# First stage of a two-layer kernel: latents in bursts of 32-row tiles, p turned in 64-row halves, division by eight heads, shorter FP4 rounding, a new step order

## The chip, the core and the metric

The kernel runs on one core of a Trainium2 chip. The metric is the device time of one execution in microseconds (us). TensorE (PE) multiplies, and its weight loads (PEld) are listed apart; VectorE (DVE), ScalarE (ACT) and GpSimd (POOL) work elementwise; SyncE (SP) issues most DMAs. TensorE writes only to PSUM, of which there are eight banks of 512 float32 columns by 128 partitions.

## What is computed

Two layers with a layer norm after each half, all in float32, on x of 16 batches x 512 tokens x 256 channels. Cut to what matters:

```python
# layer 0, attention: 16 heads of 16, lifted to 32 "latent" channels
qkv = x @ c_attn_w.T + c_attn_b ; q, k, v = heads(split(qkv))
q_lat = q @ q2l_w.T + q2l_b ; k_lat = k @ kv2l_w.T + kv2l_b ; v_lat = v @ kv2l_w.T + kv2l_b
q_lat = q_lat * cos + rotate_half(q_lat) * sin        # the same for k_lat
att = softmax(causal((q_lat @ wqk_w.T + wqk_b) @ k_lat.T * 32**-0.5))
y = (att @ v_lat) @ l2o_w.T + l2o_b                    # heads side by side
x = layernorm(x + y @ cproj_w.T + cproj_b)
# layer 0, FFN: each linear has its input and its weight rounded to FP4 in blocks of 16
#   scale = max(max|block| / 6, 1e-12); q = nearest of (0, .5, 1, 1.5, 2, 3, 4, 6) * sign * scale
x = layernorm(x + fp4_linear(silu(fp4_linear(x, w_gate)) * fp4_linear(x, w_up), w_down))
# layer 1: a recurrence over 512 tokens (state = tanh(state @ tanh(a) + x_t @ b)), then a gated FFN
```

## The kernel before

**Stages.** The first stage does attention and the FP4 FFN of layer 0, batch by batch, and writes rows of x to DRAM (`xs`). The second stage reads them back and runs the recurrence with the rest of layer 1 beside it.

**Order.** TensorE's order is the order of the program text. The other engines' instructions are ordered ahead of time by the framework's own scheduler, which may move an instruction, a DMA issue too, far ahead when nothing holds it. Attention runs in 16 x 12 slots: a slot is a batch, a group g of four heads, and one of three sets n of query blocks (`BLOCKS`: block 3, of 512 keys; block 2, of 384; blocks 1 and 0, of 256 and 128). In a slot the kernel

- forms the scores of four heads (`scores`: four products with 32 rows, each head in its own 32-row tile of TensorE and its own PSUM bank). DVE adds the mask and finds the minimum in one pass (tiles p and nm);
- runs the exponentials on ACT (`exponentials`), two heads late (`LAG = 2`);
- turns the p of the slot before, head by head, with 128x128 transposes (`turn`, tiles ps_pt and pT); ACT copies them to SBUF;
- after the third set multiplies with the values (`weighted`, tile py, four column tiles of 32) and, one slot later, divides by the sums (`divide`: DVE reciprocal rc, POOL widens it to rcx, TensorE turns it, ACT copies, DVE multiplies).

Between these, `half_slot` (eight times a slot) takes steps from a list written by hand (`PLAN`, and `PLAN_0`, `PLAN_1`, `PLAN_15` for the first, second and last batch): H heads, L latents, V values, O output projection, Q FP4 of x, U and D the FFN's two halves, W the FFN weights. "U-1.0" is the up half of token block 0 of the batch before. `TIME` holds a cost for each step, and steps are paced by it over the 96 half slots of a batch. `vector_step` hands one more piece of a waiting FP4 rounding to DVE at each half slot.

**Latents.** `latents(b, g)` has three steps for one group: q and k (two products of 64 rows and 128 columns, in the two row halves), q and k with swapped pairs (the same with bdqs and bdks), and the product with w1 (ps_qf). DVE multiplies by cos and sin, POOL adds the two, ACT adds the bias.

**PSUM.** `mm` hands out seven banks in a ring; an eighth (`ps_y`) holds py.

**FP4.** `fp4`: block maximum (L205), scale (L206), reciprocal (L207), x by the reciprocal (L210), two passes for the rounding constant (L214, L215), addition (L218), then subtraction and the product with the scale, on POOL in most calls (L219, L220).

**Weights of the recurrence.** `recurrent_weights` (28 small DMAs, five larger ones, a tanh on ACT) is called in the text at batch 2; its memory is its own, and in the profile its DMAs are issued from 17 us on.

## Time and profile before

| | |
|---|---|
| time, median of 3 runs | 2539.11 us (2538.06 to 2540.24) |
| the profiled execution: span from the first to the last instruction | 2543.7 us; no other time of that execution is recorded |
| PE, DVE, ACT, POOL busy | 2412.0, 1925.8, 1621.3, 1035.4 us |
| first score; last score | 31.7 us; 1748.2 us |
| first step of the recurrence | 1816.1 us |
| granted TensorE clock, 31 to 132 us; 354 to 1284 us | 0.87; 1.00 |

The rows of the profile name a line, an engine, an operation, its tiles and shape, how many there were, the busy time and the mean duration of one in ns, and the idle time of the engine before them with what ended it. A float32 product is two records on TensorE (two passes), a transpose one. Records of TensorE overlap, so that the distance from one start to the next says more than a duration.

### The profile page before, as it was taken

The numbers are of one execution on the slowest core, as the hardware profiler recorded it, in microseconds if no ns is written. First come the engines' busy times: TensorE is split into PE (matmuls) and PEld (weight loads), VectorE is DVE, ScalarE is ACT, GpSimd is POOL, SyncE is SP. The second block draws the span as 40 slices with busy tenths as digits, with TensorE's granted clock in tenths as the row PEclk, the third lists the DMA queues.
The fourth block names the chain that finished last, engine by engine and source line by source line (L and its number), as shares of the span: only waits on it lengthen the run. The fifth ranks groups of instructions, "written<-read, shape, count | busy, mean of one in ns | idle before, by whom it ended". The sixth has DMA issues, their size and how long they took to land.

```text
span 2543.7 us, 73791 instructions
## 1 busy us (share of the span) xinstructions
PE 2412.0 (95%) x28802; PEld 1712.7 (67%) x28802; DVE 1925.8 (76%) x5492; ACT 1621.3 (64%) x5536; POOL 1035.4 (41%) x1642
## 2 busy tenths in 40 slices
PE   7789999999999999999999999998799999999998
PEld 4455666666666666666666666655678888888885
DVE  4867888788888888888888888867756666666666
ACT  4656676676766666666666666654366666666664
POOL 4322333333333333333333333332445555555554
PEclk8889999999999999999999999989899999999999
DMA  3000000000000000000000000000111111111100
GB/s 117 24 9 6 12 24 14 16 16 12 24 14 16 16 12 24 14 16 16 12 24 14 16 14 6 16 14 9 43 32 39 37 40 41 40 38 39 36 28 27
DMA packets 58015, 61.30 MB, mean 24 GB/s; under 512 B 7873, under 2 KB 53058, under 8 KB 57666
## 3 DMA queue, kind: packets, MB, share of 16 engines
q1 hardware_dynamic: 56802, 55.54, 7.0%
q8 instruction: 226, 3.70, 0.6%
q14 instruction: 123, 1.01, 0.1%
q10 hardware_dynamic: 864, 1.05, 0.1%
HBM read 39.79 MB, written 16.78 MB: 22 GB/s over the span
## 4 chain that ended last, share of the span: by engine, by line
PE 51%; DVE 29%; ACT 10%; POOL 5%; issue 3%; DMA 1%; ACTq 0%; DVEq 0%; POOLq 0%; SPq 0%
PE u L1076 8%; DVE p L546 5%; PE ps_pt L569 5%; PE u L1036 5%; ACT p L559 4%; PE S L534 3%; PE ps_d L164 3%; DVE q_q L210 3%; ACT pT L571 3%; PE pg L164 3%; PE pu L164 2%; PE ps_h L449 2%; DVE q_sc L205 2%; DVE q_q L218 2%; PE ps_a L916 2%
## 5 line engine op out<-in xcount | busy, mean ns | idle before, releaser
L559 ACT ACTIVATE p<-p,nm 128x512 f32<-128x512 f32 (+3 forms) x1024 | 570.4, 562 | 492.3 <-DVE nm L546 488.3
L1084 ACT ACTIVATE hist<-u 64x64 f32<-64x64 f32 x2048 | 447.1, 218 | 237.4 <-PE u L1076 151.4
L546 DVE CUSTOM_DVE_ANT_0 p<-S,mask 128x512 f32<-128x512 f32 (+3 forms) x1024 | 442.9, 484 | 50.9 <-PE S L534 50.4
L1076 PEld LDWEIGHTS u<-hist,ta 128*64 128x64 f32 x8176 | 367.7, 138 | 119.9 <-ACT hist L1084 41.5
L569 PEld LDWEIGHTS ps_pt<-ident,p 128*128 128x128 f32 x2560 | 302.0, 142 | 217.3 <-issue 107.1
L571 ACT COPY pT<-ps_pt 128x384 f32<-128x384 f32 (+1 forms) x768 | 374.2, 517 | 62.3 <-PE ps_pt L569 62.1
L569 PE MATMUL ps_pt<-ident,p 128*128 128x128 f32 x2560 | 396.3, 280 | 4.5 <-DVE nm L546 3.0
L1076 PE MATMUL u<-hist,ta 128*64 128x32 f32 x8176 | 394.4, 218 | 4.6 <-ACT hist L1084 4.5
L219 POOL TENSOR_TENSOR q_q<-q_q,q_m 128x704 f32<-128x704 f32 (+1 forms) x140 | 164.1, 1172 | 372.2 <-DVE q_q L218 361.5
L534 PE MATMUL S<-kc,qr 32*128 32x512 f32 (+3 forms) x2048 | 224.1, 475 | 10.5 <-ACT qr L488 7.9
L1036 PE MATMUL u<-xt,wb 128*64 128x64 f32 x4128 | 224.9, 231 | 5.1 <-issue 5.0
L559 ACT ACTIVATION_READ_ACCUMULATOR p<-p,nm 128x1 f32 x1024 | 199.8, 195 | 0.0
L164 PE MATMUL ps_d<-wdT,hT 128*128 128x256 f32 x732 | 173.1, 386 | 13.9 <-DVE nm L546 12.1
L164 PE MATMUL pg<-wgT,xqT 128*128 128x352 f32 x512 | 177.9, 471 | 6.5 <-DVE nm L546 5.1
L483 POOL TENSOR_TENSOR qc<-qc,qs 128x512 f32<-128x512 f32 x64 | 81.5, 1273 | 235.5 <-DVE qs L482 221.1
L164 PE MATMUL pu<-wuT,xqT 128*128 128x352 f32 x512 | 173.7, 462 | 1.0 <-DVE nm L546 1.0
L1036 PEld LDWEIGHTS u<-xt,wb 128*64 128x64 f32 x4128 | 166.7, 140 | 10.3 <-issue 5.5
L600 PEld LDWEIGHTS py<-pT,vpad 128*32 128x32 f32 x5120 | 138.7, 110 | 47.0 <-issue 30.3
L600 PE MATMUL py<-pT,vpad 128*32 128x128 f32 x5120 | 162.6, 274 | 7.8 <-ACT pT L571 7.5
L164 PEld LDWEIGHTS ps_d<-wdT,hT 128*128 128x128 f32 x732 | 135.4, 192 | 37.6 <-DVE nm L546 15.4
L86 POOL TENSOR_SCALAR ve<-mv 128x2 f32<-128x2 f32 (+1 forms) x160 | 31.1, 194 | 312.4 <-DVE mv L94 309.7
L585 POOL COPY rcx<-rc 128x256 f32<-128x256 f32 x64 | 40.3, 630 | 286.9 <-DVE rc L583 260.9
(167 smaller groups left out, 4648.8 us busy)
## 6 DMA issues: line engine op xcount, KB each, us to landing
xT<-in_xT_dram SPq DMA_DIRECT2D x16, 512.0 KB
x<-in_x_dram SPq DMA_DIRECT2D x16, 512.0 KB
xs<-x SPq DMA_DIRECT2D x64, 128.0 KB
x<-xs SPq DMA_DIRECT2D x32, 256.0 KB
xm<-xs SPq DMA_DIRECT2D x32, 256.0 KB
out_dram<-o SPq DMA_DIRECT2D x64, 128.0 KB
w<-in_w_down_dram SPq DMA_DIRECT2D x2, 352.0 KB
w<-in_w_gate_dram SPq DMA_DIRECT2D x5, 128.0 KB
```

What stands on the lines that cost most here:

```text
L164: nc.tensor.matmul(dst, left, right, start=start, stop=stop)
L219: last.tensor_tensor(q, q, m, ALU.subtract)
L483: nc.gpsimd.tensor_tensor(of[k], of[k], x, ALU.add)
L534: nc.tensor.matmul(S[h][:, at : at + w], q[rs, i * P : i * P + P], k[rs, :w], start=True, stop=True,)
L546: nc.vector.tensor_tensor_reduce(out=p[:, own], in0=S[h][:, own], in1=mask[:, T - (i + 1) * P :], scale=1.0, scalar=-MASKED, op0=ALU.add, ...
L559: nc.scalar.activation(p[:, own], p[:, own], AF.Exp, bias=nm[:, u : u + 1], scale=-1.0, accum_out=sum_of[b, g][:, cb, half, h : h + 1],)
L569: nc.tensor.transpose(ps[:, at : at + P], p[:, at : at + P], ident)
L571: nc.scalar.copy(pT[:, :w], ps[:, :w])
L600: nc.tensor.matmul(py[q * 32 : q * 32 + 32, PLACE[i][1], :], vpad[b % 2][:, j, g * 4 + h, :], pt, start=j == 0 and h % 2 == 0, stop=j == i ...
L1036: nc.tensor.matmul(u[rs, k, par:n:2, bs : bs + 16], wb[:, g * 2 + k, par, half, rs], xt[:, g, at : at + n - par : 2, :], start=par == 0 an ...
L1076: nc.tensor.matmul(into[cs, :, c, :], ta[:, t % 2, g * 2 + k, cs], own[:, :, c, :], start=False, stop=True, skip_group_check=True,)
L1084: nc.scalar.activation(state[g][rs, :, r * 32 : r * 32 + 32].rearrange("p k (s b) -> p k s b", s=2), u[rs, :, t - t0, :] .rearrange("p k ( ...
```

## The change

- *Latents.* Steps are for a whole batch. `queries` (two steps, L): a spread, `spread`, of eight products of 32 rows and 64 columns into four banks; each bank times cos and times sin (eight DVE products); then 32 products of 32 rows and 32 columns that sum w1 with the cos part and w1s (new, a DMA) with the sin part into four banks, and four ACT additions of the bias. `keys` (two steps, K): a spread times cos, then a spread of the swapped weight times sin, added on POOL. bdqs and q2lbs go; the columns of wqk and the bias cabk for k are laid out anew, cabk by eight small DMAs.
- *Turning p.* Two heads at a time, each 128x128 block as two transposes of 64 rows, the row halves in different banks; four ACT copies a slot as before. All eight of a head pair's halves stand together, ahead of the slot's scores.
- *Weighted and divide.* Head h goes to column tile h, and two groups sum into one py tile; one division for eight heads.
- *FP4.* The scale moves from DVE to POOL with a yield behind it; the rounding constant takes one DVE pass (and, or) and a max inside the addition; POOL (or DVE, by `last`) repeats that max before the subtraction.
- *Order.* Turn, then scores; no lag of the exponentials; new plans, in which batch 0's heads and latents are made before the loop and every batch makes those of the next one.
- *Memory.* One xT buffer in place of two; caw in the short-lived pool; `recurrent_weights` is called after the first stage, with its pool opened there.

```diff
-        nc.vector.scalar_tensor_tensor(sc, sc, 1.0 / 6.0, tiny[:rows, :nb], ALU.mult, ALU.max)
+        nc.gpsimd.tensor_scalar(sc, sc, 1.0 / 6.0, 1e-12, ALU.mult, ALU.max)
+        yield
         nc.vector.reciprocal(inv, sc)
-        if n > C:
-            yield
+        yield
...
-        nc.vector.tensor_scalar(m.bitcast(U32), q.bitcast(U32), 0x7F800000, None, ALU.bitwise_and)
-        nc.vector.tensor_scalar(m, m, 1.0, 1.5 * 2.0**22, ALU.max, ALU.mult)
-        if n > C:
-            yield
-        nc.vector.tensor_tensor(q, q, m, ALU.add)
+        nc.vector.tensor_scalar(
+            m.bitcast(U32), q.bitcast(U32), 0x40800000, MAGIC_BITS, ALU.bitwise_and, ALU.bitwise_or
+        )
+        yield
+        nc.vector.scalar_tensor_tensor(q, m, MAGIC, q, ALU.max, ALU.add)
+        last.tensor_scalar(m, m, MAGIC, None, ALU.max)
         last.tensor_tensor(q, q, m, ALU.subtract)
...
+        def spread(name, left, hs):
+            ps = [mm(name) for _ in range(4)]
+            for r in range(4):
+                rs = slice(r * 32, r * 32 + 32)
+                for c in range(2):
                     nc.tensor.matmul(
+                        ps[r][c * 64 : c * 64 + 64, :], left[rs, r * 64 : r * 64 + 64],
+                        hs[rs, c, :], start=True, stop=True, skip_group_check=True,
+                    )
+            return ps
+        def times(ps, bias, table, tag, bufs):
+            x = att.tile([P, T], F32, tag=tag, name=tag, bufs=bufs)
+            nc.vector.scalar_tensor_tensor(x, ps, bias, table, ALU.add, ALU.mult)
+            return x
+        def queries(b):
+            X = spread("ps_q", bd["bdq"], heads_of.pop((b, 0)))
+            rotated = []
+            for r in range(4):
+                rotated.append([
+                    times(X[r], col("q2lb"), table, tag, 4) for table, tag in ((cos, "qc"), (sin, "qs"))
+                ])
+            yield 1.0
+            Y = [mm("ps_qf") for _ in range(4)]
+            for u, w in enumerate((w1, w1s)):
+                for a in range(4):
+                    rs = slice(a * 32, a * 32 + 32)
+                    for c in range(4):
+                        cs = slice(c * 32, c * 32 + 32)
+                        nc.tensor.matmul(
+                            Y[a][cs, :], w[rs, rs], rotated[c][u][rs, :],
+                            start=u == 0, stop=u == 1, skip_group_check=True,
+                        )
+            for a in range(4):
+                qr = query_of[b, a] = att.tile([P, T], F32, tag="qr", name="qr", bufs=QR)
+                nc.scalar.activation(qr, Y[a], AF.Identity, bias=wqkb)
+            yield 1.9
+        def keys(b):
+            hs = heads_of.pop((b, 1))
+            for a, ps in enumerate(spread("ps_k", bd["bdk"], hs)):
+                key_of[b, a] = times(ps, col("kv2lb"), cos, "kc", KC)
+            yield 1.0
+            for a, ps in enumerate(spread("ps_ks", bd["bdks"], hs)):
+                x = times(ps, col("kv2lbs"), sin, "ks", 2)
+                nc.gpsimd.tensor_tensor(key_of[b, a], key_of[b, a], x, ALU.add)
+            yield 1.0
...
         def turn(n, p):
-            w = sum(i + 1 for i, _ in BLOCKS[n]) * P
-            ps = mm("ps_pt")
-            for at in range(0, w, P):
-                nc.tensor.transpose(ps[:, at : at + P], p[:, at : at + P], ident)
-            pT = ptp.tile([P, T], F32, tag="pT", name="pT")
-            nc.scalar.copy(pT[:, :w], ps[:, :w])
-            return pT
+            w = sum(i + 1 for i, _ in BLOCKS[n])
+            done = []
+            for h in (0, 2):
+                halves = [mm("ps_pt").rearrange("p (u n t) -> p u n t", u=2, t=64) for _ in range(2)]
+                for u in range(2):
+                    for at in range(w):
+                        for r in range(2):
+                            rs = slice(r * 64, r * 64 + 64)
+                            nc.tensor.transpose(
+                                halves[r][:, u, at, :], p[h + u][rs, at * P : at * P + P], ident[rs, rs],
+                            )
+                pT = ptp.tile([P, 2, NT, 2, 64], F32, tag="pT", name="pT")
+                for r in range(2):
+                    nc.scalar.copy(pT[:, :, :w, r, :], halves[r][:, :, :w, :])
+                done.append(pT.rearrange("p u n r t -> p u (n r t)"))
+            return done
...
+                rT = att.tile([P, T], F32, tag="rT", name="rT")
+                nc.scalar.copy(rT, ps)
+                nc.vector.tensor_tensor(
+                    y_of[b][:, a1, :], py.rearrange("p i t -> p (i t)"), rT, ALU.mult
+                )
...
+        PLAN = ["U-2.3", "U-2.3", "O-1", "D-2.2", "D-2.2", "O-1", "Q-1.0", "H1", "U-1.0", "H1", "Q-1.1", "L1", "U-1.0", "U-1.0", "D-2.3", "U-1.1", "Q-1.2", "U-1.1", "V1", "H1", "U-1.2", "Q-1.3", "D-2.3", "H1", "K1", "U-1.2", "U-1.1", "D-1.0", "K1", "U-1.2", "L1", "D-1.1", "D-1.0", "D-1.1", "U-1.3", "V1"
         ]
...
+            for slot in slots + [None] * 2:
...
+                if len(pTs) == 2 * len(BLOCKS):
+                    weighted(*of, pTs)
+                    pTs = []
+                if before:
+                    of = before[0][:2]
+                    pTs += turn(before[0][2], [p for p, _ in before[1]])
                 if slot:
                     b, g, n = slot
...
                     tiles = scores(b, g, n)
                 for h in range(4):
                     beside.half_slot()
-                    if before:
-                        pTs.append(turn(before[0][2], before[1][h]))
                     if slot:
-                        behind.append((*slot, h, *tiles[h]))
-                        ps.append(tiles[h][0])
-                    while len(behind) > (LAG if slot else 0):
-                        exponentials(*behind.pop(0))
+                        exponentials(*slot, h, *tiles[h])
...
+    ta, wb, wc, bout = recurrent_weights()
     wts = ctx.enter_context(tc.tile_pool(name="wts2", bufs=1))
```

## The prediction

> **What bounds the kernel now.** I read the page's busy shares by slice first, then busy time per engine in a steady stretch, then that stretch's groups by shape, then TensorE's order of time.
>
> ```profile
> PE   7789999999999999999999999998799999999998
> PEclk8889999999999999999999999989899999999999
> ```
>
> Slices 4 to 27 are the steady part of the first stage: TensorE is at 90% or more in each, at full granted clock.
>
> ```profile
> 421.00:1381.00 960.00, 932.65 (x7644) 632.80 (x7644) 796.52 (x2327) 640.67 (x1908) 341.73 (x397) 1.00 0.05 16
> ```
>
> Columns: stretch, length, busy PE, weight loads, DVE, ACT, POOL. How many batches is that? Scores of form 32x512 are 32 records a batch (4 groups, 4 heads, 2 passes):
>
> ```profile
> L534 PE MATMUL S<-kc,qr 32*128 32x512 f32 x288 | 41.1, 639 | 4.9 <-ACT qr L488 4.9
> L569 PE MATMUL ps_pt<-ident,p 128*128 128x128 f32 x1444 | 220.8, 277 | 0.4 <-DVE nm L546 0.4
> L621 DVE TENSOR_TENSOR yT<-py,rT 64x256 f32<-64x256 f32 x72 | 30.3, 421 | 13.1 <-ACT rT L616 12.2
> L206 DVE SCALAR_TENSOR_TENSOR q_sc<-q_sc,tiny 128x44 f32<-128x44 f32 x36 | 20.7, 574 | 0.9
> L215 DVE TENSOR_SCALAR q_m<-q_m 128x704 f32<-128x704 f32 x36 | 18.8, 521 | 0.3
> ```
>
> 288 records are 9 batches, so a batch takes 106.7 us, and per batch PE is busy 103.6, DVE 88.5, ACT 71.2, POOL 38.0. TensorE is the bound, DVE 15 us behind. A busy TensorE is pipelined, so I price its work by the distance from one start to the next:
>
> ```profile
> 1014.62 0.49 PE L569 MATMUL ps_pt<-ident,p 128*128 128x128 f32 x3
> 1014.95 0.82 PE L333 MATMUL ps_h<-ident,hq 128*128 128x128 f32 x6
> 1015.60 1.02 PE L486 MATMUL ps_qf<-qc,w 128*128 128x512 f32 x2
> 1016.47 0.49 PE L569 MATMUL ps_pt<-ident,p 128*128 128x128 f32 x3
> ...
> 1020.18 1.14 PE L534 MATMUL S<-kc,qr 32*128 32x512 f32 x8
> 1021.25 0.55 PE L569 MATMUL ps_pt<-ident,p 128*128 128x128 f32 x3
> ...
> 1025.84 0.69 PE L467 MATMUL ps_q<-heads,bdq 64*128 64x512 f32 x1
> 1025.93 0.69 PE L467 MATMUL ps_k<-heads,bdk 64*128 64x512 f32 x1
> ...
> 1026.98 0.55 PE L569 MATMUL ps_pt<-ident,p 128*128 128x128 f32 x3
> 1027.46 0.69 PE L467 MATMUL ps_qs<-heads,bdqs 64*128 64x512 f32 x1
> ...
> 1028.73 2.42 PE L600 MATMUL py<-pT,vpad 128*32 128x128 f32 x80
> 1031.08 1.34 PE L534 MATMUL S<-kc,qr 32*128 32x384 f32 x8
> ```
>
> One 128x128 turn advances TensorE by 0.33/3 = 0.11 us. Eight score records in four row tiles take 1.07 for two passes of 512 columns, so row tiles run side by side. Eighty py records in four column tiles take 2.35, 0.029 each, a quarter of 0.11, so column tiles do too. One group's latents cost 1.14 (ps_q, ps_k) + 1.27 (turned pair) + 0.87 (ps_qf) = 3.28.
>
> **Turning p in halves.** Before: 160 turns a batch x 0.11 = 17.6 us of TensorE. After: 320 records, each 64 rows and 64 moving columns, two in different row halves and different banks. The trace has no such record. Lower bound: halves fully side by side, 160 x 0.055 = 8.8. Upper: one after the other, each as long as a whole one now, 35.2. I take the rate of py, 320 x 0.029 = 9.4, the nearest row for small records in tiles: saving 8.2. The copies to pT keep number and size (L571), the 64-element runs cost nothing where ACT already writes 16-element runs at the same price (vpad 372 ns, rT 376 ns, both 256 wide).
>
> What speaks against it is the weight load. In the trace sixteen loads of 32 x 128 and their products fill 1.06 us (the 256-and-128 scores, 1011.45 to 1012.51). The Trainium skill, "TensorE: Matmul & The Clock Gate", section "LDWEIGHTS (loading the stationary operand)", says that a load lasts columns / 1.2 GHz whatever its rows: sixteen in series would be an estimated 1.71 us, and 320 loads of 128 columns in series 34.1 us a batch, so that the batch would end near 119 and not 95. The measured 1.06 is shorter than 1.71, so loads into different rows overlap; the row decides.
>
> **Latents in bursts.** Before 4 x 3.28 = 13.1 us of TensorE a batch. After: three spreads (q, k, turned k) of eight 32x64 products, and 32 products of 32x32 in place of ps_qf and turned q. If all tiles run side by side a spread is two passes as the score burst is, 1.07, and the 32 products are twice that, 2.1: 5.3 in all. If column tiles under one row tile run in turn: 3 x 2.1 + 4 x 2.1 = 14.7. I take 5.3, since py shows column tiles and S row tiles side by side; saving 7.8 (the other end costs 1.6). DVE's 16 products stay (qc, kc, qs, ks: start to start 0.66 each in the trace). POOL loses four additions of 1.27 us (L483), 5.1.
>
> **Division by eight heads.** DVE 8 x 0.421 becomes two 128x512 products, 2 x 0.687 (L507, same width, also from PSUM): -2.0. Four reciprocals of 0.233 become two: -0.3. ACT -0.3, TensorE and POOL equal. All off the path.
>
> **FP4.** DVE loses L206 and L215, per batch 4 x (0.574 + 0.285) + 4 x (0.521 + 0.290) = 6.7. POOL gains a small scale step (0.19 by L86, eight a batch: 1.5) and a pass of max: between 0.48 for 256 (xn L879) and 1.4 to 1.7 for 704 (L220, L219), 7.6 a batch. DVE falls to 88.5 - 9.0 = 79.5, POOL rises to 42. The added wait: the reciprocal on DVE now waits for POOL, with all of DVE's queue behind it. One half slot lies between (106.7/96 = 1.1 us), POOL's longest instruction is 1.7: from nothing to 0.8 each, I count 0.5 a batch.
>
> **Order.** Scores now come after the turn of the whole previous slot, and exponentials lose their lag of two. The queries step puts eight products, 5.3 us, on DVE at once and holds four of seven banks; masks of the next scores queue behind: from nothing to 5.3, I take 2.5. Each of two key steps puts 2.6 there: 0.5 each. With 0.5 for the reciprocals, new waits are 4.0 a batch. Single xT buffer: the next load is asked for when its last reader has ended, some 2 slots ahead of the first "H1" (0 to 3 us, none taken).
>
> Middle batches: 106.7 - 8.2 - 7.8 + 4.0 = 94.7, 12.0 less. Batches 1 to 14: -168. Batch 0 is paced by weight quantizing as well (clock 0.87 there), TensorE loses 8.2 + 9.8 + 3.5 of heads; I count -12 (0 to -21). Before the first score two more head steps (1.76 each) and 12 more DVE products (7.9) come: +8 (4 to 15, with eight small loads of cabk on SP where two of q2lbs took 2.30). Batch 15: -10 (0 to -18). The recurrent weights move from the start to the stage's end: 28 issues on SP of about 0.6 (ta 592 ns, wb 604) and five more, 20 us, before the xs write of the last tokens, behind whatever frees that memory, and ACT's tanh of ta waits for them with its gate tanhs and copies behind it. The stretch from the last py at 1760 to the first recurrence at 1816 covers most: +6 (0 to 20).
>
> Sum on the profiled execution's span: 2543.7 - 168 - 12 + 8 - 10 + 6 = 2367.7. The span is 4.6 above the median of three runs, 2539.1, so **2363**.
>
> **The rivals.** *Columns not side by side* (0.12): latents cost 1.6 more instead of 7.8 less; 94.7 + 9.4 = 104.1, -2.6 x 14 = -36, the other terms -8: about 2495. For: no record mixes row and column tiles. Against: each alone does run so.
> *Bursts cost their length* (0.12): waits of 13 us a batch, 5.3 + 2 x 2.6 on DVE and 2.5 of ACT's qr (4 x 0.63), banks held throughout. 103.7: -42 - 8, about 2489. For: DVE and TensorE are then within 11 us. The skill's "TensorEngine Tiling (Array Packing)", section "PSUM Bottleneck", warns that tiling speeds up TensorE and not the emptying of PSUM; before the change the trace has DVE 15 us under TensorE, so it isn't seen there.
> *Slower: the slot becomes a loop* (0.16). Turn needs the last exponential of the slot before, scores follow the turn, exponentials follow the masks. In series: second pair's turn 0.5, scores 1.07, first mask 0.67, four exponentials 2.4 (384 wide, 1033.34 to 1035.75) to 3.6 (256 and 128), say 3.0. ACT's pT copies are 16 x 0.587 + 32 x 0.481 = 24.8 a batch, its exponentials 16 x (0.721 + 0.608 + 0.516 + 0.402) = 36.0, which leaves 10.4 of 71.2: a slot has 2.1 of copies and 0.9 of other ACT work. Sum 8.2; a slot now takes 106.7/12 = 8.9. So it decides once foreign DVE work ahead of the masks exceeds 0.7 a slot. DVE's masks are 16 x (0.674 + 0.552 + 0.421 + 0.287) = 30.9, so it has (79.5 - 30.9)/12 = 4.0 of that; with 1.2 ahead a batch is 12 x 9.4 = 112.8, +6.1 x 14 - 8: about 2616. Against: the copies can run under scores and first mask (1.7), leaving 6.5.
>
> **How the numbers follow.** The forecast has 0.58, with own range 2300 (no new waits: 2307) to 2430. With the first two rivals, 0.82 faster by over 0.2% (about what a measurement of this kernel can tell from no change); 0.02 within 0.2%, 0.16 slower. The range reaches up to the first two rivals, 2300 to 2495.
>
> **What would show it.** ps_pt records of 64 rows about 0.03 apart; spreads of about 1.1; a batch near 95 with PE still at 90% or more; DVE near 80 busy. Wrong if spreads take 2 or more, if PE falls under 85% with waits on the mask's nm, or if the stretch from the last py to the first recurrence exceeds 65.

## The result and the profile after

The changed kernel takes **2631.28 us** (median of 4 runs, 2627.81 to 2635.27) against 2539.68 of the kernel before on the same chip: ratio 1.0358 [1.0343, 1.0372], slower by 91 us where 176 less was forecast. The profiled span is 2630.8, 87.1 longer than the 2543.7 of before.

First the page's slices:

```profile
PE   7879899999998999999999999988589999999998
PEclk8889999899999999999999999998889999999999
```

PE's busy share looks as it did. Two stretches of the first stage (columns: stretch, length, busy PE, weight loads, DVE, ACT, POOL, granted clock, DMA):

```profile
514.10:1520.70 1006.60, 939.13 (x9721) 618.26 (x9721) 728.41 (x2106) 637.74 (x1891) 425.93 (x487) 0.94 0.05 16
...
1168.00:1172.00 4.00, 3.60 (x12) 2.70 (x12) 0.98 (x2) 0.42 (x3) 1.84 (x2) 0.60 0.00 0
```

The long stretch holds 9 batches: 111.8 us each, with PE busy for 93%. What is new is the clock, 0.94 where the steady stretch of before had 1.00. In that stretch 28 windows of 3.4 or 6.8 us, 122.9 us in all, ran at half clock; the last line is one of them. DVE fell to 728.41 / 9 = 80.9 a batch (79.5 forecast), POOL rose to 47.3 (42 forecast).

The groups by shape of the same stretch (count | busy us, mean ns | idle before it and what ended it):

```profile
L555 PE MATMUL S<-kc,qr 32*128 32x512 f32 x289 | 82.4, 670 | 12.5 <-DVE ks L475 9.5 <-ACT heads L457 3.0
L595 PE MATMUL ps_pt<-ident,p 64*128 64x64 f32 x2880 | 132.0, 229 | 10.1 <-ACT p L579 3.9 <-DVE ks L475 3.1 <-DVE h L315 2.1
L524 PE MATMUL ps_o<-cpT,yT 128*128 128x256 f32 x144 | 48.7, 484 | 29.7 <-DVE yT L643 29.7
L207 POOL TENSOR_SCALAR q_sc<-q_sc 128x44 f32<-128x44 f32 x36 | 13.7, 380 | 279.8 <-DVE q_sc L206 279.0
L209 DVE RECIPROCAL q_inv<-q_sc 128x44 f32<-128x44 f32 x36 | 15.3, 426 | 13.7 <-POOL q_sc L207 13.7
L220 POOL TENSOR_SCALAR q_m<-q_m 128x704 f32<-128x704 f32 x36 | 71.1, 1976 | 80.1 <-DVE q_q L219 79.3
```

The output projection (ps_o) waits 29.7 / 9 = 3.3 us a batch for the divided tile yT, which it never did in the steady stretch of before:

```profile
L501 PE MATMUL ps_o<-cpT,yT 128*128 128x256 f32 x144 | 34.1, 379 | 0.0
```

DVE's reciprocal now waits for POOL's scale pass, and the POOL pass of max takes 1.98 us for 704 columns, not the 1.4 to 1.7 of the forecast.

TensorE's order of time (start, length, count, idle before):

```profile
964.30 2.44 PE L555 MATMUL S<-kc,qr 32*128 32x512 f32 x8 [0.30 <-ACT heads L457]
...
974.07 1.20 PE L595 MATMUL ps_pt<-ident,p 64*128 64x64 f32 x32
975.20 1.16 PE L555 MATMUL S<-kc,qr 32*128 32x384 f32 x8
...
1012.62 1.11 PE L466 MATMUL ps_ks<-heads,bdks 32*64 32x512 f32 x16
1013.66 0.86 PE L595 MATMUL ps_pt<-ident,p 64*128 64x64 f32 x13
...
1164.11 0.66 PE L640 MATMUL ps_r<-ident,rcx 128*128 128x128 f32 x4
1164.60 0.60 PE L524 MATMUL ps_o<-cpT,yT 128*128 128x256 f32 x2
1168.36 2.93 PE L524 MATMUL ps_o<-cpT,yT 128*128 128x256 f32 x6 [3.16 <-DVE yT L643]
```

The pieces do what was forecast: 32 half turns advance TensorE by 1.13 us, 0.035 each (0.029 forecast), and a spread takes 1.04 (1.07). But the 512-wide scores take 2.4 us at 964.30, where they took 1.07. Single records of the traces show the difference: at 1020.18 of the kernel before, the four heads' records start 7 ns apart; at 964.30 each starts 0.05 to 0.36 us behind the last, and those that the trace gives a releaser for wait for ACT (tiles heads, xqT and pT). TensorE counts as busy all the while. And the output projection follows 0.5 us behind ps_r, whose result still has to pass through ACT and DVE to become its operand yT. VectorE at the same place:

```profile
1162.26 0.89 DVE L211 SCALAR_TENSOR_TENSOR q_q<-h,q_inv 128x704 f32<-128x704 f32 x1
1163.18 0.53 DVE L215 TENSOR_SCALAR q_m<-q_q 128x704 uint32<-128x704 uint32 x1
1163.75 0.89 DVE L219 SCALAR_TENSOR_TENSOR q_q<-q_m,q_q 128x704 f32<-128x704 f32 x1
1164.56 0.55 DVE L567 CUSTOM_DVE_ANT_0 p<-S,mask 128x384 f32<-128x384 f32 x1
...
1167.61 0.69 DVE L643 TENSOR_TENSOR yT<-py,rT 128x512 f32<-128x512 f32 x1 [1.07 <-ACT rT L642]
1171.33 0.69 DVE L530 TENSOR_TENSOR x<-ps_o,x 128x512 f32<-128x512 f32 x1 [3.02 <-PE ps_o L524]
```

Three rounding passes and four masks stand ahead of yT, then ACT's copy; afterwards DVE idles 3.02 us for TensorE. Neither engine is full there; they wait for each other in turn.

Where the 87.1 us lie, by the first scores of the batches: before the first score +7.6; batch 0 +2.2; batch 1 +4.1; batches 2 to 14 13 x 4.97 = +64.6; batch 15, up to its last py, +1.9; from there to the first step of the recurrence +4.3 (56.2 to 60.4), behind it +2.3.

### The profile page after: what moved, and what is told of

Its sections match the earlier page's. It is cut to its first block, busy times and chain, and to the rows that moved or that the text cites. A ratio compares the mean times of both kernels' runs of the same rounds, so it can differ in the third digit from the quotient of the medians.

```text
span 2630.8 us, 81289 instructions
## 1 busy us (share of the span) xinstructions
PE 2410.7 (92%) x32514; PEld 1686.1 (64%) x32514; DVE 1797.8 (68%) x5080; ACT 1614.6 (61%) x5506; POOL 1196.7 (45%) x1826
## 4 chain that ended last, share of the span: by engine, by line
PE 57%; DVE 19%; POOL 11%; ACT 8%; issue 3%; DMA 1%; SPq 1%; ACTq 0%; POOLq 0%; DVEq 0%
PE u L1091 8%; PE S L555 6%; ACT p L579 5%; PE pg L165 5%; PE ps_d L165 5%; PE u L1051 4%; PE py L625 4%; PE pu L165 4%; PE ps_pt L595 3%; POOL q_m L220 3%; DVE p L567 2%; DVE q_q L211 2%; PE ps_a L931 2%; PE ps_k L931 2%; PE ps_kv L931 2%
## 5 line engine op out<-in xcount | busy, mean ns | idle before, releaser
L600 ACT COPY pT<-ps_pt 128x384 f32<-128x384 f32 (+1 forms) x768 | 340.3, 526 | 237.7 <-PE ps_pt L595 236.1
L555 PE MATMUL S<-kc,qr 32*128 32x512 f32 (+3 forms) x2048 | 310.9, 492 | 23.5 <-DVE ks L475 13.8
L220 POOL TENSOR_SCALAR q_m<-q_m 128x704 f32<-128x704 f32 (+1 forms) x140 | 195.4, 1396 | 218.2 <-DVE q_q L219 188.3
L207 POOL TENSOR_SCALAR q_sc<-q_sc 128x44 f32<-128x44 f32 (+2 forms) x143 | 46.9, 328 | 520.0 <-DVE q_sc L206 512.0
L595 PEld LDWEIGHTS ps_pt<-ident,p 64*128 64x128 f32 x5120 | 191.6, 140 | 123.5 <-ACT p L579 71.1
L595 PE MATMUL ps_pt<-ident,p 64*128 64x64 f32 x5120 | 240.9, 231 | 24.1 <-ACT p L579 13.6
L165 PE MATMUL pg<-wgT,xqT 128*128 128x352 f32 x512 | 213.4, 546 | 5.3 <-DVE ks L475 3.1
L555 PEld LDWEIGHTS S<-kc,qr 32*128 32x128 f32 x2048 | 157.2, 189 | 78.7 <-DVE ks L475 26.3
L165 PE MATMUL pu<-wuT,xqT 128*128 128x352 f32 x512 | 187.5, 492 | 4.1 <-DVE nm L567 4.1
L165 PEld LDWEIGHTS pg<-wgT,xqT 128*128 128x128 f32 x512 | 102.0, 218 | 101.9 <-ACT pT L600 20.3
```

The source lines that it names most:

```text
L165: nc.tensor.matmul(dst, left, right, start=start, stop=stop)
L220: last.tensor_scalar(m, m, MAGIC, None, ALU.max)
L555: nc.tensor.matmul(S[h][:, at : at + w], q[rs, i * P : i * P + P], k[rs, :w], start=True, stop=True,)
L595: nc.tensor.transpose(halves[r][:, u, at, :], p[h + u][rs, at * P : at * P + P], ident[rs, rs],)
L600: nc.scalar.copy(pT[:, :, :w, r, :], halves[r][:, :, :w, :])
```

## The experiments

All were timed beside the kernel before, on several chips. "Batch" is the mean of batches 2 to 14. The three last columns split TensorE's start-to-start distances in batches 5 to 12, us a batch: each counts as *work* up to 0.87 ns for each moving column and 95 ns more (512 columns advance 0.53 us in the trace), what exceeds that as *waits*, and half of what falls into half clock as *clock*.

The split is rough, in three ways. Kernels that give TensorE the products of the change in another order or with other steps on the other engines have 95.6 to 98.3 of work, so differences of 1 to 2 us in that column say little. Score records that start one by one, as at 964.30, count as work: the scores have 13.0 of it before, 13.0 in e8, 15.3 in e6 and 18.1 in the changed kernel, and what is above 13 is a wait. *Clock* is the most that half clock can cost, since TensorE would have waited through a part of it anyway.

| kernel | us | against before [95%] | batch | work | waits | clock |
|---|---|---|---|---|---|---|
| before | 2540 | 1 | 106.7 | 103.0 | 3.5 | 0.0 |
| e4 + halves | 2592.66 | 1.0205 [1.0187, 1.0222] | 110.1 | 103.1 | 6.0 | 0.6 |
| e5 + rounding | 2691.55 | 1.0599 [1.0582, 1.0617] | 117.1 | 103.7 | 9.6 | 3.4 |
| e15, its scale on DVE | 2597.67 | 1.0218 [1.0203, 1.0233] | 110.4 | 104.4 | 5.4 | 0.6 |
| e8 + slot order | 2529.14 | 0.996 [0.9946, 0.9975] | 106.4 | 103.1 | 2.9 | 0.2 |
| e11, its own plan reordered | 2798.48 | 1.1014 [1.0997, 1.103] | 126.6 | 104.7 | 13.0 | 8.3 |
| e13 + latents | 2616.03 | 1.0291 [1.0274, 1.0309] | 110.5 | 99.2 | 7.3 | 3.6 |
| e9 = e13 + rounding | 2682.34 | 1.0556 [1.0537, 1.0575] | 114.8 | 100.2 | 9.8 | 4.5 |
| e6 = e9 + slot order | 2638.06 | 1.0384 [1.0369, 1.04] | 111.8 | 100.0 | 6.5 | 5.5 |
| **after** = e6 + halves | 2631.28 | 1.0358 [1.0343, 1.0372] | 111.7 | 96.4 | 8.7 | 6.4 |
| e1, old rounding | 2613.78 | 1.0296 [1.0279, 1.0313] | 111.1 | 95.8 | 7.4 | 8.3 |
| e17, scale on DVE | 2597.30 | 1.0218 [1.0203, 1.0234] | 109.2 | 96.4 | 7.7 | 5.1 |
| e18 = e17, half bursts | 2596.59 | 1.023 [1.0209, 1.0251] | 109.1 | 99.4 | 6.5 | 3.4 |
| e2, scores first | 2931.43 | 1.154 [1.152, 1.1561] | 131.4 | 97.1 | 16.3 | 17.9 |
| e3, interleaved | 2756.93 | 1.0856 [1.084, 1.0873] | 119.6 | 97.4 | 13.6 | 8.5 |

**First theories: the rounding's chain, or the slot as a loop.** Four kernels. e1 puts the old rounding back into the changed kernel:

```diff
-        nc.gpsimd.tensor_scalar(sc, sc, 1.0 / 6.0, 1e-12, ALU.mult, ALU.max)
+        nc.vector.scalar_tensor_tensor(sc, sc, 1.0 / 6.0, tiny[:rows, :nb], ALU.mult, ALU.max)
...
```

> The changed kernel with the FP4 rounding of before (scale and both constant passes on DVE, no extra POOL pass). Theory ORDER (the slot is a loop: last exponential, turn, scores, mask, exponentials; TensorE waits in it, and the clock falls in the gaps): the time stays within 25 us of 2631, since DVE only gets 6 us busier. Rival FP4 (DVE stands behind POOL's scale, 3.5 us a batch, and rounded tiles come late through POOL's max pass of 1.98 us): about 8 us a batch come back, 2510 or less. Rival BURSTS (DVE's cos and sin products in one piece and banks held by them): no change, 2620 to 2650.

It gained 17 us of the 91, so the rounding is a part here and not the whole. e2 and e3 try the slot's order in the changed kernel: e2 forms the scores ahead of the turn, e3 also turns in pairs within the slot, with the lag of two.

```diff
-                if before:
-                    of = before[0][:2]
-                    pTs += turn(before[0][2], [p for p, _ in before[1]])
                 if slot:
...
                     tiles = scores(b, g, n)
+                if before:
+                    of = before[0][:2]
+                    pTs += turn(before[0][2], [p for p, _ in before[1]])
```

> The changed kernel with the slot's scores ahead of the turn of the slot before (two blocks of the loop swapped, nothing else). ORDER: masks and exponentials of a slot no longer wait for the last exponential of the one before; 4 to 10 us a batch come back, 2480 to 2570, clock nearer to 1.00. FP4: no change, 2610 to 2650. BURSTS: no change, or a loss by banks, 2620 to 2700.

```diff
...
                 for h in range(4):
                     beside.half_slot()
+                    if before and h % 2 == 0:
+                        pTs += turn(before[0][2], [p for p, _ in before[1]], h)
                     if slot:
-                        exponentials(*slot, h, *tiles[h])
+                        behind.append((*slot, h, *tiles[h]))
+                    while len(behind) > (2 if slot else 0):
+                        exponentials(*behind.pop(0))
...
```

> The changed kernel with scores first, the turns as two pairs between the steps (after the first and the fifth half slot) and the exponentials two heads late, as before the change. ORDER: most of the waits go, 95 to 100 us a batch, 2380 to 2460. FP4: as e2 or 2600. BURSTS: 2560 or more.

Both are much slower. The waits of e2 from 514 to 1520 us (engine, tile, releaser: us in total, times, longest) say why it is:

```profile
PEld ps_pt L595 <- DVE nm L567: 112.5, 68, 4.3
PE ps_pt L595 <- DVE nm L567: 101.9, 61, 4.2
```

Four score banks and four turn banks are eight, the ring has seven: the turn's last bank waits for a mask of the same slot, and nothing behind it can go. With the turn first, its banks come free with ACT's copies, for which the scores then wait, but for less. So the new order is the better one of the two for this ring, and the remedy that the loop theory asked for was wrong. e3 has no such row: its largest wait is the one on yT, 3.5 us a batch, and waits on masks are spread over several tiles (6.7).

**Each part by itself in the kernel before.** e4 turns in 64-row halves, two heads at h = 0 and h = 2:

```diff
...
-                    if before:
-                        pTs.append(turn(before[0][2], before[1][h]))
+                    if before and h % 2 == 0:
+                        pTs.append(turn(before[0][2], before[1][h : h + 2]))
```

> The kernel before with only the 64-row turn (in pairs of heads, after the first and the fifth half slot). If the halves run side by side and TensorE is the bound there, 160 x (0.11 - 0.037) = 11.7 less 4 for the DVE and ACT that are then close, so 6 to 11 us a batch: 2370 to 2445. If the turn in halves were itself the loss of the changed kernel: above 2540.

It is 53 us slower. The turn got cheaper (ps_pt 19.5 to 13.9 us a batch), yet work stayed at 103.1 and waits rose by 2.5. The bursts change between 64-row and 128-row records, and the distances at these borders are longer by about 0.09 us: from pu to ps_pt 0.39 us, where it was 0.30. That each pair holds two banks until its copies would account for the waits, but no run shows it by itself. e8 takes the slot's order alone:

```diff
-        LAG = 2
+        LAG = 0
...
+                if before:
+                    pTs += [turn(before[0][2], before[1][h]) for h in range(4)]
+                if slot:
                     tiles = scores(b, g, n)
...
-                    if before:
-                        pTs.append(turn(before[0][2], before[1][h]))
```

> The kernel before with the new order of a slot alone: its four whole turns in a burst ahead of the scores, and each exponential without the lag of two heads. Latents, division, rounding and plan as before. Theory of the order (the slot becomes a loop: turn, scores, masks, exponentials, turn of the next slot, with eight banks asked of a ring of seven at once): 2600 to 2680. Theory of the latents' bursts (the spreads of four banks and the eight cos and sin products behind them are what holds banks): 2530 to 2555.

```profile
514.00:1520.00 1006.00, 986.77 (x8052) 669.86 (x8052) 834.24 (x2449) 683.74 (x2015) 363.88 (x420) 1.00 0.05 16
```

Clock 1.00, 12 us (0.4%) **faster** than before: this is the one kernel that beats both. The loop that the forecast priced as its slow case is not there, with whole turns and the old latents. e5 takes the new rounding alone:

```diff
-        nc.vector.scalar_tensor_tensor(sc, sc, 1.0 / 6.0, tiny[:rows, :nb], ALU.mult, ALU.max)
+        nc.gpsimd.tensor_scalar(sc, sc, 1.0 / 6.0, 1e-12, ALU.mult, ALU.max)
+        yield
...
+        last.tensor_scalar(m, m, MAGIC, None, ALU.max)
```

> The kernel before with the new rounding alone. VectorE saves about 6 us a batch, GpSimd has the max pass more. Where the quantized tiles are not waited for (the kernel before has fillers between), within 8 us of 2540; if the longer chain is waited for here too, 2550 to 2565, as the 17 us in the changed kernel were.

151 us, far outside both expectations. Its waits on VectorE, and what TensorE then waits for (514 to 1520 us):

```profile
DVE q_inv L210 <- POOL q_sc L208: 55.7, 43, 3.9
DVE x L102 <- POOL rstd L90: 51.3, 34, 2.8
DVE q_sc L207 <- POOL hq L223: 29.7, 9, 3.3
PEld ps_pt L572 <- DVE nm L549: 49.1, 53, 2.5
PE ps_d L166 <- DVE nm L549: 18.9, 8, 2.4
```

A pass of 0.38 us stands in POOL's queue behind passes of 1.98, 1.69 and more; DVE waits up to 3.9 us for it with all masks behind it; the masks hold the banks. e15 moves this one pass back to VectorE in e5, e17 in the changed kernel:

```diff
-        nc.gpsimd.tensor_scalar(sc, sc, 1.0 / 6.0, 1e-12, ALU.mult, ALU.max)
+        nc.vector.tensor_scalar(sc, sc, 1.0 / 6.0, 1e-12, ALU.mult, ALU.max)
```

> The kernel before with the new rounding, but with the division of the block maxima by 6 on VectorE in place of GpSimd (44 columns, so a short pass); nothing else. In the kernel before with the new rounding VectorE waited 54.6 us in 1000 (5.8 a batch) for that pass, which stands behind other passes in GpSimd's queue. Theory of the queue: the wait goes, and the time with it, 2691 to 2590-2620; what is left is GpSimd's added max pass, behind which rstd and the rounded tile come later. Theory of the longer chain of steps (five instead of three): nothing gained, 2680 to 2700.

> The changed kernel with the division of the block maxima by 6 on VectorE in place of GpSimd; nothing else. VectorE waited 3.5 us a batch for that pass. If VectorE's waiting sets the pace, 10 to 30 us faster, 2600 to 2621, about as the old rounding as a whole (2614). If VectorE's waits only fill time in which it has nothing else, 2625 to 2637.

94 and 34 us come back; on VectorE the pass takes 0.27 us in e15 and 0.18 in e17, and no wait of q_inv on POOL is left. The same misplaced pass costs 6.7 us a batch in the kernel before and 2.5 in the changed one; the two differ in more than the slot order, and which difference matters was not tested. e15 is still 56 us behind. VectorE's waits on rstd and hq, behind POOL's added max pass, are larger there than in the kernel before, which has 30.8 on rstd (the last row) and none on hq; that they are what costs the time is not shown:

```profile
DVE x L102 <- POOL rstd L90: 54.9, 36, 2.3
DVE q_sc L207 <- POOL hq L223: 33.0, 9, 3.7
```

```profile
DVE x L100 <- POOL rstd L88: 30.8, 38, 1.2
```

**The changed kernel with parts put back.** e6 has whole turns in the burst, e9 also the slot order of before, e13 also the old rounding, so that the latents with their division, plan and stage end are left.

```diff
             for h in (0, 2):
-                halves = [mm("ps_pt").rearrange("p (u n t) -> p u n t", u=2, t=64) for _ in range(2)]
...
+                    ps = mm("ps_pt")
+                    for at in range(0, w * P, P):
+                        nc.tensor.transpose(ps[:, at : at + P], p[h + u][:, at : at + P], ident)
...
```

> The changed kernel with the earlier kernel's whole 128 by 128 turns put back, still in one burst at the slot's start and still four banks of it; everything else as changed. If the narrow halves are a gain of TensorE's time that shows (theory: work on TensorE sets the pace), this is slower by the 4 to 7 us a batch by which 160 whole turns (17.6) exceed the halves (11 to 13): 2690 to 2730. If waits for banks and for neighbours set the pace, much of the added work goes into time that TensorE waits anyway, and the clock rises with it: 2620 to 2670. If the halves with their switches between the 64-row and 128-row modes are what went wrong, it is faster: below 2600.

```diff
-                    pTs += turn(before[0][2], [p for p, _ in before[1]])
...
+                        pTs.append(turn(before[0][2], before[1][h]))
+                    while len(behind) > (2 if slot else 0):
+                        exponentials(*behind.pop(0))
```

> The changed kernel with the order of a slot and the whole turns of the kernel before (one turn a half slot, a lag of two heads), so that latents in bursts, division by eight heads, rounding and the recurrent weights at the stage's end are left of the change. Theory of the order: the latents' gain on TensorE (12.3 to 6.0 us a batch) shows, 2450 to 2500. Theory of the latents' bursts: they hold the banks whatever the order, 2560 to 2640. The new rounding alone is worth about +17 in the changed kernel and would be in this one too.

e13's edit is that of e1 in e9.

> The changed kernel with the slot order, the whole turns and the rounding of the kernel before: the latents in bursts, the division by eight heads, their plan and the recurrent weights at the stage's end are all that is left. If each part is harmless by itself and only the lengthened rounding hurts (it alone cost the kernel before 151 us), this is about 2682 - 151 = 2531. If the latents' bursts and their plan by themselves lose the cover of the chain from division to gate products, the 5 us a batch on yT stay: 2600 to 2640.

These make a path from one kernel to the other: latents +75 (e13), rounding +66 (e9), slot order -44 (e6), halves -7 (after). A part's price depends on what is there already: the rounding costs 151 alone and 17 in the changed kernel, the halves 53 alone and -7 here. The halves save 3.6 us of work a batch in the burst and give back 3.1 in waits and clock. The latents save 3.8 of work and bring 3.8 of waits and 3.6 of clock. e13's waits:

```profile
PEld ps_o L525 <- DVE yT L634: 29.4, 9, 3.3
PE ps_o L525 <- DVE yT L634: 25.8, 9, 2.9
```

The wait on yT comes with the latents' plan, under either order. In the old plan two latent and two head steps stood ahead of the first output projection, a latent step between the two, and four more between the second and U-1.0; the latent ones are gone. The profiled run of e13 is 70 us longer than that of before: 50 are in batches 2 to 14 (13 x 3.8), the rest at the start (6), in batches 0 and 1 (4), batch 15 (7) and behind the first step of the recurrence (4). The single xT buffer is not the reason: in no trace of the two kernels does TensorE wait for its load.

**Is it the plan?** e11 puts the kernel before into the same position, by its plan's order alone; the other kernels move steps of the changed kernel's plan (e12 and e16 with the old rounding, e19 with the scale on VectorE).

```diff
-        PLAN = ["L0.1", "L0.1", "U-2.3", "U-2.3", "H0", "H0", "O-1", "D-2.2", "L0.1", "D-2.2", "O-1", ...
+        PLAN = ["U-2.3", "U-2.3", "O-1", "D-2.2", "D-2.2", "O-1", "Q-1.0", "L0.1", "L0.1", "L0.1", "U-1.0", "H0", ...
```

> The kernel before, nothing changed but the order of its plan for the middle batches: output projection, quantizing and the gate products stand as close behind the division as in the changed kernel (two U-2.3, O-1, two D-2.2, O-1, Q-1.0, three latent steps, U-1.0), and the latents of the groups 2 and 3 and the heads stand behind them. Theory of the lost cover: the same stalls on yT and on the quantized tile appear here, 3 to 6 us a batch: 2580 to 2620. Theory of the banks: the latents are not in bursts here, so it stays at 2540 to 2555.

```profile
PEld ps_o L501 <- DVE yT L621: 27.0, 8, 3.4
PE ps_o L501 <- DVE yT L621: 23.8, 8, 3.0
PE ps_qf L486 <- POOL qc L483: 21.4, 16, 3.1
```

The same wait of 3 us a batch appears in a kernel without bursts, so an output projection close behind its division does cost it. But 126.6 a batch is far more than that (clock 8.3, waits 13.0): moving the later latents also brought new waits within them, as the last row shows, and of the scores on them. So e11 shows the wait, and not what it costs. The other direction:

```diff
-        PLAN = ["U-2.3", "U-2.3", "O-1", "D-2.2", "D-2.2", "O-1", "Q-1.0", "H1", "U-1.0", "H1", "Q-1.1", "L1", ...
+e7      PLAN = ["U-2.3", "U-2.3", "D-2.2", "D-2.2", "H1", "O-1", "H1", "O-1", "Q-1.0", "Q-1.1", "U-1.0", "L1", ...
+e10,12  PLAN = ["U-2.3", "U-2.3", "D-2.2", "D-2.2", "H1", "O-1", "H1", "O-1", "V1", "H1", "Q-1.0", "Q-1.1", "H1", "D-2.3", "D-2.3", "L1", "U-1.0", ...
+e16     PLAN = ["U-2.3", "D-2.2", "U-2.3", "H1", "D-2.2", "O-1", "H1", "O-1", "V1", "D-2.3", "H1", "Q-1.0", "Q-1.1", "D-2.3", "L1", "U-1.0", ...
+e19     PLAN = ["U-2.3", "U-2.3", "D-2.2", "H1", "O-1", "Q-1.0", "D-2.2", "O-1", "H1", "U-1.0", "Q-1.1", "L1", ...
```

> The changed kernel with the two steps of the output projection moved behind the second D-2.2 and one H1 each in the plan of the middle batches, so that they no longer follow straight on the division whose product they read; nothing else moves but the quantizing steps that follow them. If the 3.4 us a batch that ps_o waits for yT are real and leave with nothing in their place, 13 batches give 44 us and the clock that was lost around them some more: 2560 to 2585. If the stream of TensorE is held as a whole by the banks and by VectorE, the wait moves to the next place: 2615 to 2640.

> The changed kernel with another order of the same steps in the plan of the middle batches: the output projection behind both D-2.2 and one step of heads each, then all of V1, H1, D-2.3 and the first L1 between the second O-1 and the three U-1.0; the rest follows in its old order. Theory of the lost cover: the 30 small latent steps used to stand between the division, the output projection, the quantizing and the gate products, which wait for each other through VectorE and GpSimd; with the steps gone the same chain stands in front of TensorE. Then the 5.1 us of stalls and the 1.9 us of half clock in the first group of every batch go, 13 batches of 5 to 7: 2540 to 2570. Theory of the banks held by the spreads: the stalls move, as they did when the output projection alone was moved: 2610 to 2640.

> The plan of e10_plan and the rounding of the kernel before in the changed kernel. The old rounding took 17 us off the changed kernel. Theory of the lost cover: its chain is one VectorE step shorter and without the GpSimd pass, so where the chain no longer stands in front of TensorE it is worth less than that, and VectorE's longer passes cost: within 10 us of e10_plan on either side. Theory of VectorE's load (banks held because VectorE comes late): it is slower than e10_plan by 10 to 20.

> The changed kernel with the rounding of before (2614 as measured) and a plan of the middle batches in which no step follows at once on the one whose result it reads: the two steps of each D stand two or three others apart, the output projection behind D-2.2 and a step of heads, the first U-1.0 behind V1, H1, D-2.3 and L1. In e10_plan the waits on yT and on the quantized tile were gone, and 6.5 us a batch on hT had come, where the two steps of a D stood together. Theory of the order of the plan: both are gone now, 11.5 us of stalls fall to some 5, and half of the lost clock comes back: 2500 to 2560. Theory that the stream is short of work between VectorE's results wherever they stand: 2600 to 2650.

> The changed kernel with the scale pass on VectorE as in e17_after_scale_dve (2597), and the first twelve steps of the middle batches' plan in another order, all later ones as they were: D-2.2 and a step of heads now stand between the division and the first output projection, Q-1.0 right behind that one, the second D-2.2, the second output projection and the second step of heads ahead of U-1.0. Nothing is moved across a burst of the latents. If the 3.1 us on yT and the 2.5 us of half clock in the first group are the waiting for the division and can be filled, 13 batches of 3 to 5.6: 2525 to 2557. If the wait only moves on to the quantized tile or to the masks, 2585 to 2610.

| | us | against before [95%] | batch | the largest waits of TensorE by the same split, us a batch |
|---|---|---|---|---|
| e7 | 2636.12 | 1.0381 [1.0363, 1.0398] | 111.8 | xq from POOL 4.4, hT from ACT 2.8 |
| e10 | 2697.05 | 1.0611 [1.0595, 1.0627] | 116.4 | hT 6.5, xqT 1.4 |
| e12 | 2699.42 | 1.0624 [1.0609, 1.064] | 117.3 | hT 7.0, exponentials 2.5 |
| e16 | 2663.31 | 1.0476 [1.0461, 1.0492] | 114.4 | exponentials 3.4, qs products 3.2 |
| e19 | 2676.27 | 1.0539 [1.0505, 1.0574] | 114.7 | yT 2.5, exponentials 2.4 |

e7, e10, e12 and e16 did take the wait on yT away, and in e16 the first group of a batch has 1.1 us of waits in all; in each the wait came back elsewhere. In e19 even yT stayed late, because VectorE now waited up to 3.0 us for the rT copy on ACT. My hand-made plans were all no better than the plan of the change. That another order would give the 3 us back is not shown.

**Bursts of half the size.** e18 cuts each spread of e17 in two: `rows` is (0, 1), then (2, 3) a step later.

```diff
-            ps = [mm(name) for _ in range(4)]
-            for r in range(4):
+            ps = {r: mm(name) for r in rows}
+            for r in rows:
...
```

> e17_after_scale_dve (2597) with every spread of the latents cut in two steps of two banks, each followed by the two to four VectorE products that read them, and a half slot or more between; the 32 small products stay one step. In e17 the waits of TensorE that end with a ks product are 1.9 us a batch, and masks come behind up to eight products in a row on VectorE. Theory of the held banks: most of the 1.9 and the clock behind it go, less 0.7 us a batch for four more pairs of switches between the row modes: 2565 to 2590. Theory that the bursts' length does no harm: the switches alone, 2597 to 2615. The wait on yT is not touched by it.

No difference in time: 2.9 us a batch of waits and clock go, and 2.9 of work come. Eight records of two row tiles take 1.02 us, as long as sixteen of four (1.5 us a batch for k and ks), and the 32 small products took 4.0 in place of 2.4. The two halves of q still stood back to back on TensorE, so the cut was tested on k and ks alone.

## Why the prediction was wrong

**What held.** The columns do run beside row tiles: a spread is 1.04 us (1.07 forecast), so the first rival falls; the 32 small products take 2.28 (2.1). Latents went from 12.25 to 6.0 us of work (7.8 less forecast, 6.3 measured). So the signs that the forecast named for the turn, the spreads and DVE all came, and the time went the other way. DVE came to 80.9 (79.5), the start cost 7.6 (8), the stage's end 6.6 (6). On the weight load the row was the better guide: 320 half turns take 12.9 us a batch, where the rule of the Trainium skill ("TensorE: Matmul & The Clock Gate", section "LDWEIGHTS (loading the stationary operand)") made an estimated 34.1 in series; in this trace, loads into different rows overlap.

**The step that failed: TensorE's saved work taken for time.** The sum took 16.0 off a batch for turn and latents and added 4.0 of waits. Measured, turn and latents fell by 12.9, four fifths of that, but the scores took 5.1 more and all else 1.2, so that work fell by only 6.6 (103.0 to 96.4); waits rose by 5.1 (3.54 to 8.66), and the clock, for which the sum had no term, took up to 6.4: together +4.9 in batches 5 to 12. The new waits were priced at 4.0; with those of the scores they came to 10.2. In the terms of the sum:

- *Turn, 9.4.* ps_pt takes 12.9, 6.6 less than its 19.5; but the scores behind each turn rose from 13.0 to 18.1, because their records start one by one: of the late starts that the trace gives a releaser for, about half name ACT's copies of the turn (pT). The rise is 0 in e8, with the same order, whole turns and the old latents, and 2.3 in e6, with whole turns. Of the 8.2, 3.6 are work that a whole turn would have cost (e6), and 0.2 a batch arrive in the time.
- *New waits, 4.0.* The reciprocals were priced at 0.5; the scale pass costs 2.5 in the changed kernel (e17) and 6.7 in the kernel before (e15). "One half slot lies between" compared it with one POOL instruction; there is a queue of three. The latents' bursts were priced at 2.5 + 2 x 0.5; halving two of the three spreads changed nothing (e18). The wait of the output projection on yT, 3.3 to 3.5, was not in the list at all: the new plan has no latent steps there, and the sum priced the steps it took out by their length alone. That these steps had covered the division fits e13 and e11, which have the wait under the old slot order; no plan tried gave the time back.
- *Clock.* The half-clock windows come behind stretches in which little of the array is fed (last section): waits, and scores that start one by one. In the first group of a batch 5.1 us of waits stand beside 1.9 of clock, in the whole batch 8.7 beside 6.4.
- *Batch 0 and batch 15,* -12 and -10, came out at +2.2 and +1.9; they rest on the same two savings.

**The rivals.** Of the second one, bursts that cost their length, little shows: 1.8 us a batch of the changed kernel's waits end with a ks product, and halving k and ks gained nothing. The slow one gave 2616 and had the right sign and nearly the size, but as a whole its mechanism is not what happened: the order that it blamed gains 12 us in the kernel before and 44 in e9. One link of it, scores held behind the turn's copies, is there with the halves. The mark set for failure, PE under 85%, would have missed it: PE is busy 93%, because long records at half clock and scores that start one by one count as busy.

What stays open is why the waits of the changed kernel hold out against every other plan tried, and how much of the 75 us of the latents is plan and how much the bursts' 8 products in a row on VectorE. Halves and the new order together, with the old latents and rounding, were not run.

## What to carry to other kernels

When a change takes small steps out of an in-order stream, list what each of them covered: the dependent pair that they stood between may meet. Before a short pass goes to another engine, read that engine's queue ahead of it, and what stands behind the waiting instruction. Where row tiles are to run side by side, ask what lets them start together: one at a time they count as busy and feed a quarter of the array. And where an engine is close to its bound, the first test of a composite change is each part alone: here, of halves, rounding, slot order and latents, one was a gain by itself, and it was the one under suspicion.

## What the runs showed of the hardware that had not been expected

- The clock goes by how much of the array is fed more than by idle time. Count for each record its moving columns, times the share of 128 rows and of 128 columns that it uses, and add up what starts in each of the 3.4 us windows on whose borders the clock changes. In the twenty traces, from 400 to 1600 us, 561 windows have under 1400, and 547 of them were followed by half clock; 5894 have over 1800, and 2 were; of the 573 between, 165. The kernel before has a median of 3584 and nothing under 1920. Of the 6317 windows at full clock the best single limit misplaces 76 by this count and 249 by idle time. Eight 512-wide score records count 1024, in 1.07 us side by side (1020.18 of the kernel before) and in 2.37 us one by one (964.30 of the changed one), all of it busy time.
- So the clock falls for a window of 3.4 us after far less than 3.4 us of idle. Of the 28 half-clock stretches in the changed kernel, 9 followed a gap of 3.2 to 3.6 us, and 19 followed 3.4 us in which the gaps were 0.74 us or shorter, 0.3 to 1.4 in sum. 95% of the windows at full clock had at most 0.47 of idle ahead of them; no sharp limit of idle time shows, for a window of before had 1.33 and kept the full clock. (The ends of records are modelled.) The Trainium skill, "TensorE: Matmul & The Clock Gate", section "HAM oscillation — how this bites in real kernels", asks for no gap over some 3.4 us; here that would not be enough. Its next section, "A second HAM failure mode: psum-queue depth-cycling", tells of many small gaps between bursts; these rows have such gaps, but the count above separates the windows better.
- A POOL pass of max over 128x704 takes 1.98 us and the subtraction behind it 1.69 in e5, where the rows of the profile before for such passes had 1.4 to 1.7.
- A spread of 32-row, 64-column products takes the same time for two row tiles (8 records, 1.02 us in e18) as for four (16 records, 1.04 us in the changed kernel).
